# Head softmax: two blocks' denominators as one product, half of it behind the values; experts' sums in a shared bank, openings 16 units ahead

## The chip, the cores and the metric

The kernel runs on one core of a Trainium2 chip. The metric is the device time of one execution in microseconds (us), as the median of the runs shown. The core has five engines with queues of their own: PE (matrix products; PEld are its weight loads), DVE (vector), ACT (activations), POOL (elementwise work and some transfers) and SP (transfers).

## The reference

The program is a two-layer hybrid network on x of shape (2, 1024, 128) in float32. Only its last two steps matter here: an attention whose softmax runs over the heads, and a feed-forward layer of eight experts that is applied before it and again after it.

```python
# _L1_attn_b: 16 heads of 8
qkv = x @ w_qkv + b_qkv                    # -> q, k, v: (b, 16, n, 8)
dp = jnp.einsum('bhqd,bhkd->bhqk', q, k) * SCALE
attn = jax.nn.softmax(dp, axis=1)          # over the heads
w_avg = jnp.einsum('bhqk,bhkd->bhqd', attn, v)
out = w_avg.reshape(b, n, 128) @ w_proj + b_proj

# _L1_ffn: for each of 8 experts, FFN = 512
h = jax.nn.silu(x @ wg) * (x @ wu)
acc = acc + h @ wd
```

x takes the result of each step as an addition: x = x + ffn(x), x = x + attn_b(x), x = x + ffn(x).

## The kernel before

x lies in the on-chip memory as 16 tiles of 128 tokens (`x_res`). Earlier stages (latent attention, state space, linear attention) fill the first half of the execution. Then come `experts_ffn(g, w, [2])` (the experts on four tiles at once), `heads_and_experts(g, w, [6, 7], [0, 1, 2, 3, 4, 5])`, which the change touches, and `experts_ffn(g, w, [3])`.

`heads_and_experts` weaves two streams. The first is the head softmax. A block is 128 queries by 128 keys of all 16 heads; there are 2 x 8 x 8 = 128 blocks. For each block PE forms the scores in four banks (`products`, L1148), DVE takes the maxima over the heads (L1159) and subtracts them (L1165), and ACT takes the exponentials (L1168). The sum over 16 heads is then made in two steps: a transfer from SP's queue copies the lower eight heads (L1174), a transfer from POOL's queue adds the upper eight onto them (L1178), and PE adds the eight remaining slices with eight products by the identity (L1183). DVE inverts (L1188), POOL multiplies all heads by the inverse (L1193), and PE weighs the values (L1199). Eight blocks give one tile of 128 queries: ACT copies the result out (L1294), PE projects it (L1263) and DVE adds it to x (L1272). `finished` counts these tiles.

The second stream, `ExpertStream`, works on chunks of two tiles. A chunk is opened by five steps (norm statistics on DVE, root on ACT, inverse on DVE, norm on POOL, transposes on PE), and then gives 32 units (8 experts x 4 slices of FFN). A unit is two gate products on PE (L997), a SiLU on ACT (L1004), a product on DVE (L1012) and the output product (L1023). The outputs of two units at a time are added up in a bank, which DVE adds to x (L1032).

The order is written out by hand (`manual_schedule`): each engine executes the loop's instructions in the order of the code. Chunk 6 is worked off beside `preparation(0)`, the projections q, k, v of the first batch; chunk 7 and then 0 to 5 go through the block loop, two units an iteration. `aside(place)` slips in one step of an opening, or of `preparation(1)`, at its place. An opening begins when few enough units are left (the second number in `side`) and enough tiles are finished (the first). In iteration i the loop treats scores of block i+1, exponentials of i+1, the upper transfer of i, the denominators of i-1, the inverse and the multiplication of i-2 and the values of i-3.

Buffers: scores four banks once (`h_ps_s`), one bank `h_ps_d` for denominators, outputs and projection alike, one for the weighed values (`h_po`), two for gates (`e_pgu`); `h_e` has four buffers of 8 KB a partition, `h_a` two, `h_e2` three.

Of the kernel before, what the change touches and what calls it, by code (L numbers as in the profile page):

```python
# [19 lines left out]
P = 128  # L20
B = 2
L = 1024
# [932 lines left out]
class ExpertStream:  # L955

    NE, FC = 8, 4

    def __init__(self, g, w, work, ps):
        self.g, self.w, self.work, self.ps = g, w, work, ps
        self.units, self.fresh, self.gated, self.ready, self.sums = [], [], [], [], []

    def tokens(self, chunk):
        return self.g.x[:, 2 * chunk : 2 * chunk + 2, :]

# [20 lines left out]
    def products(self):  # L988

        nc, w = self.g.nc, self.w  # L990
        for _ in range(2):
# [16 lines left out]
    def multiply(self):  # L1008
        nc = self.g.nc
        for chunk, e, fc, pgu, sg in self.gated:  # L1010
            h = self.work.tile([P, 2 * P], F32, name="e_h", bufs=6)
            nc.vector.tensor_mul(h, sg, pgu[:, 1, :])  # L1012
            self.ready.append((chunk, e, fc, h))
        self.gated = []

    def outputs(self, po):

        nc = self.g.nc
        if self.ready:
            two, self.ready = self.ready[:2], self.ready[2:]  # L1020
            for t in range(2):
                for k, (_, e, fc, h) in enumerate(two):
                    nc.tensor.matmul(  # L1023
                        po[:, t, :], h[:, bass.ts(t, P)], self.w["Wd"][:, e, fc, :], start=(k == 0), stop=(k == 1)
                    )
            self.sums.append((two[0][0], po))

    def add(self):

        for chunk, po in self.sums:  # L1030
            xt = self.tokens(chunk)
            self.g.nc.vector.tensor_add(xt, xt, po[:, 0:2, :])  # L1032
        self.sums = []
# [12 lines left out]
def heads_and_experts(g, w, first, second):  # L1046
# [4 lines left out]
    with ExitStack() as es:  # L1051
# [10 lines left out]

        keep = one.tile([P, K], F32, name="h_keep")
# [12 lines left out]
        ex = ExpertStream(g, w, ework, ps_e)  # L1076
        qzs, kTs, vs = {}, {}, {}

        def preparation(b):
# [3 lines left out]
            u = seq.tile([P, TPB, D], F32, name="h_u", bufs=1)  # L1083
            uT = seq.tile([P, L], F32, name="h_uT", bufs=1)
            qzs[b] = seq.tile([P, K, L], F32, name="h_qz")
# [6 lines left out]
            for t in range(0, TPB, 2):  # L1092
                yield "pool", lambda t=t: ln.apply(u, (t, t + 1))

# [5 lines left out]

            def transposes(n):
                pt = ps_e.tile([P, 4, P], F32, name="e_pgu")
                for t in range(4):
                    nc.tensor.transpose(pt[:, t, :], u[:, 4 * n + t, :], g.ident)
                nc.scalar.copy(uT[:, bass.ts(n, 512)], pt.rearrange("p a b -> p (a b)"))

            def query(n):
                cols = bass.ts(n, 512)
                pm = ps_e.tile([P, 4, P], F32, name="e_pgu").rearrange("p a b -> p (a b)")
                nc.tensor.matmul(pm, w["w_qkv2"][:, 0:P], uT[:, cols], start=True, stop=True)  # L1110
                for k in range(K):
                    nc.scalar.activation(  # L1112
                        qzs[b][:, k, cols], pm, AF.Identity, bias=keep_b[:, k : k + 1], scale=keep[:, k : k + 1]
                    )

# [16 lines left out]
            for step in (transposes, key, query, value):  # L1132
# [10 lines left out]
        def products(b, qb, kb):  # L1143

            s = ps_s.tile([P, J, 512], F32, name="h_s")
            for j in range(J):
# [4 lines left out]
                    qzs[b][quad, :, bass.ts(qb, P)],  # L1151
# [10 lines left out]
        def exponentials(heads, m):  # L1162

            e = work.tile([P, H, P], F32, name="h_e", bufs=4)
# [7 lines left out]
        def lower(e):  # L1172
            e2 = work.tile([P, 8, P], F32, name="h_e2", bufs=3)
            nc.sync.dma_start(out=e2, in_=e[:, 0:8, :])  # L1174
            return e2
# [4 lines left out]
        def denominators(e2):  # L1180
            pd = ps_d.tile([P, 4, D], F32, name="h_pd")[:, 0, :]
            for k in range(8):
                nc.tensor.matmul(pd, g.ident, e2[:, k, :], start=(k == 0), stop=(k == 7))  # L1183
            return pd

        def inverse(pd):
            r = work.tile([P, P], F32, name="h_r")
# [3 lines left out]
        def normalize(e, r):  # L1191
            a = work.tile([P, H, P], F32, name="h_a")
            nc.gpsimd.tensor_mul(a, e, r.unsqueeze(1).to_broadcast([P, H, P]))  # L1193
            return a

        def weigh(kb, a, po):
            for k in range(K):
                for j in range(J):
# [4 lines left out]
                        start=(kb == 0 and k == 0),  # L1203
                        stop=(kb == TPB - 1 and k == K - 1),
                    )
# [3 lines left out]
        side = [(2 * c + 2, 8, ex.opening(c)) for c in second]  # L1209
        side.insert(1, (0, 24, preparation(1)))  # L1210
        side = [(0, 8, ex.opening(c)) for c in first[1:]] + side
# [28 lines left out]
        with tc.manual_schedule(engines=ALL):  # L1240
            for _, step in ex.opening(first[0]):
                step()
            for place, step in preparation(0):
                step()
                if place != "act":
                    po = ps_d.tile([P, 4, D], F32, name="h_pd")
                    ex.outputs(po)
                    ex.add()
# [4 lines left out]
            e_, e2_, d_, a_ = {}, {}, {}, {}  # L1253
            oT = po = None
            for i in range(-1, n + 4):
                if i + 1 < n:
                    heads = products(*blocks[i + 1])
                r = inverse(d_.pop(i - 2)) if 0 <= i - 2 < n else None
                if ex.ready or oT is not None:
                    pd = ps_d.tile([P, 4, D], F32, name="h_pd")  # L1260
                    ex.outputs(pd)
                    if oT is not None:
                        nc.tensor.matmul(pd[:, 2, :], oT, w["w_proj2"], start=True, stop=True)  # L1263
                ex.multiply()
                if not aside("pe"):
                    ex.products()
                if i + 1 < n:
                    m = maxima(heads)
                ex.add()
                if oT is not None:  # L1270
                    xt = g.x[:, finished, :]
                    nc.vector.tensor_add(xt, xt, pd[:, 2, :])  # L1272
# [3 lines left out]
                if i + 1 < n:  # L1276
                    e_[i + 1] = exponentials(heads, m)
                    e2_[i + 1] = lower(e_[i + 1])
                aside("dve")
                if 0 <= i - 1 < n:  # L1280
# [238 lines left out]
```

## Time and profile before

| what | us |
|---|---|
| median of 3 runs (lowest to highest) | 2267.17 (2259.31 to 2271.51) |
| the profiled execution | 2268.1 |
| its span in the profile | 2266.4 |
| first gate product of `heads_and_experts` (PE L997) | 1188.66 |
| first and last maxima of the block loop (DVE L1159) | 1252.30 and 2139.74 |
| PE busy over the span | 1974.6 |
| DVE busy over the span | 1694.8 |
| POOL busy over the span | 908.5 |
| POOL's multiplication by the inverse (L1193), 128 times | 583.0, mean 4.555 |

Times in the profile are counted from the start of the span. A row of the timeline or of a chain gives start, length, engine, line, and how many instruction records it holds; in brackets stands how long the engine was idle before it and what ended that. A group's row gives the count, busy time, the mean in ns, and the idle time before its instructions.

### The profile page before, as it was taken

To read this page: it belongs to the slowest core of one execution; us is meant where nothing else is said; L and a number is where in the kernel's file an instruction comes from. 1 tells how busy PE (TensorE), PEld (TensorE's weight loads), DVE (VectorE), ACT (ScalarE), POOL (GpSimd) and SP (SyncE) were. 2 spreads that over 40 slices of the span, in tenths; PEclk is the share of its full clock that TensorE was granted. 3 is DMA by queue.
4 is the path that set the end of the run, shared out by engine and by line. 5 is a ranking of instruction groups with operands and counts; after the bars stand their busy time and mean duration, and the time that the engine had idled before them with its cause. 6 is when DMAs were issued, how large, how long until landed. Compare 5 with 4: busy or idle time off the path is not lost. (4 is left out here: it accounts for less than half of the span.)

```text
span 2266.4 us, 36372 instructions
## 1 busy us (share of the span) xinstructions
PE 1974.6 (87%) x14832; PEld 1157.8 (51%) x14832; DVE 1694.8 (75%) x2054; ACT 1188.3 (52%) x1497; POOL 908.5 (40%) x480
## 2 busy tenths in 40 slices
PE   7679888779967558899898798988999999999999
PEld 4223343223334123344446576766777777777753
DVE  5966767897856789945323898988898899998822
ACT  1026512366624637734223675756777777777722
POOL 0013300063401020100101578887787777787720
PEclk9889988889988769999999899999999999999999
DMA  3000000395730577500000455565555555555500
GB/s 88 1 1 1 1 1 6 88 224 142 174 112 10 138 186 167 131 0 0 1 0 1 121 150 154 151 162 139 160 150 154 149 150 152 156 153 143 153 11 5
DMA packets 73798, 220.15 MB, mean 97 GB/s; under 512 B 9184, under 2 KB 19872, under 8 KB 73504
## 3 DMA queue, kind: packets, MB, share of 16 engines
q1 hardware_dynamic: 54736, 149.40, 22.0%
q0 software_dynamic: 18432, 67.12, 15.1%
q8 instruction: 116, 1.90, 0.4%
q10 hardware_dynamic: 464, 1.33, 0.3%
q14 instruction: 50, 0.41, 0.1%
HBM read 78.35 MB, written 5.24 MB: 37 GB/s over the span
## 5 line engine op out<-in xcount | busy, mean ns | idle before, releaser
L1193 POOL TENSOR_TENSOR h_a<-h_e,h_r 128x2048 f32<-128x2048 f32 x128 | 583.0, 4555 | 140.6 <-PE h_po L1199 100.2
L1159 DVE TENSOR_REDUCE h_m<-h_s 128x128 f32<-128x2048 f32 x128 | 293.2, 2291 | 70.9 <-PE h_s L1148 70.9
L1183 PE MATMUL h_pd<-h_e,ident 128*128 128x128 f32 x2048 | 264.7, 283 | 37.9 <-DMA h_e<-h_e 24.6
L1165 DVE TENSOR_TENSOR h_e<-h_s,h_m 128x2048 f32<-128x2048 f32 x128 | 292.4, 2284 | 2.3 <-DVE h_m L1159 0.6
L1168 ACT ACTIVATE h_e<-h_e 128x1024 f32<-128x1024 f32 x256 | 256.6, 1049 | 66.8 <-DVE h_e L1165 60.7
L1183 PEld LDWEIGHTS h_pd<-h_e,ident 128*128 128x128 f32 x2048 | 242.4, 194 | 80.6 <-DVE x_res L1032 47.6
L1004 ACT ACT_TABLE_LOAD x110 | 141.1, 1283 | 162.2 <-PE e_pgu L997 162.0
L356 POOL TENSOR_SCALAR_AFFINE_SELECT a_pT<-a_pT 128x256 f32<-128x256 f32 x120 | 125.9, 1072 | 223.3 <-ACT a_pT L353 137.5
L917 DVE TENSOR_TENSOR e_h<-e_sg,e_pu 128x512 f32<-128x512 f32 x128 | 87.0, 684 | 162.1 <-PE e_pu L910 136.4
L261 DVE TENSOR_REDUCE a_nm<-a_s 128x2 f32<-128x1024 f32 (+7 forms) x144 | 168.1, 1217 | 39.1 <-PE a_s L252 24.2
L912 ACT ACTIVATE e_sg<-e_pg 128x512 f32<-128x512 f32 x128 | 76.1, 596 | 191.1 <-PE e_pg L909 172.6
L1023 PEld LDWEIGHTS h_pd<-Wd,e_h 128*128 128x128 f32 x1024 | 125.1, 191 | 95.1 <-DVE e_h L1012 78.1
L353 ACT ACTIVATE a_pT<-a_st 128x1024 f32<-128x1024 f32 (+3 forms) x176 | 129.9, 792 | 72.8 <-PE a_st L339 72.0
L746 DVE TENSOR_TENSOR_SCAN s_h<-s_a,s_h 128x1024 f32<-128x1024 f32 x64 | 149.0, 2328 | 20.1 <-ACT s_a L714 15.4
L1148 PE MATMUL h_s<-h_qz,h_kT 32*128 32x512 f32 x1024 | 148.9, 651 | 17.1 <-DVE h_e L1165 12.1
L997 PE MATMUL e_pgu<-e_uT,Wg 128*128 128x256 f32 x512 | 155.0, 385 | 2.6 <-ACT h_qz L1112 2.1
L910 PE MATMUL e_pu<-e_uT,Wu 128*128 128x512 f32 x256 | 139.1, 626 | 19.5 <-DVE e_h L917 19.5
L1023 PE MATMUL h_pd<-Wd,e_h 128*128 128x128 f32 x1024 | 149.7, 288 | 6.6 <-DVE e_h L1012 3.6
L1178 POOL DMA_DIRECT2D h_e<-h_e x128 | 114.9, 898 | 100.8 <-DVE h_m L1159 48.7
L243 PE MATMUL a_s<-a_latT,a_qT 32*128 32x512 f32 (+3 forms) x768 | 117.7, 590 | 41.3 <-DVE a_nm L261 39.2
L997 PE MATMUL e_pgu<-e_uT,Wu 128*128 128x256 f32 x512 | 153.2, 381 | 0.0
L1168 ACT ACT_TABLE_LOAD x111 | 142.4, 1283 | 12.0 <-issue 7.7
(268 smaller groups left out, 3235.8 us busy)
## 6 DMA issues: line engine op xcount, KB each, us to landing
h_e<-h_e SPq DMA_DIRECT2D x128, 512.0 KB, 3.8
h_e<-h_e POOLq DMA_DIRECT2D x128, 512.0 KB, 4.5
s_a<-s_steps SPq DMA_DIRECT2D x64, 512.0 KB, 4.9
s_h<-s_steps SPq DMA_DIRECT2D x64, 512.0 KB, 6.4
s_steps<-s_gate SPq DMA_DIRECT2D x8, 256.0 KB, 3.6
Wg<-in_Wg_dram SPq DMA_DIRECT2D x8, 256.0 KB, 6.0
Wu<-in_Wu_dram SPq DMA_DIRECT2D x8, 256.0 KB, 5.9
Wd<-in_Wd_dram SPq DMA_DIRECT2D x8, 256.0 KB, 6.1
```

The lines of the kernel that those rows point to most:

```text
L261: nc.vector.tensor_reduce(nm[:, half, i, h : h + together], s[:, :, :n], AX.X, ALU.max, negate=True)
L746: nc.vector.tensor_tensor_scan(h, a, h, 0.0, ALU.mult, ALU.add)
L910: nc.tensor.matmul(pu, w["Wu"][:, e, f], opened[n], start=True, stop=True)
L997: nc.tensor.matmul(pgu[:, k, :], w[name][:, e, f], uT, start=True, stop=True)
L1004: nc.scalar.activation(sg, pgu[:, 0, :], AF.Silu)
L1023: nc.tensor.matmul(po[:, t, :], h[:, bass.ts(t, P)], self.w["Wd"][:, e, fc, :], start=(k == 0), stop=(k == 1))
L1148: nc.tensor.matmul(s[:, j, :].rearrange("p (k q) -> p k q", k=K), kTs[b][quad, bass.ts(kb, P)], qzs[b][quad, :, bass.ts(qb, P)], start=Tru ...
L1159: nc.vector.tensor_reduce(m, heads.rearrange("p h q -> p q h"), AX.X, ALU.max)
L1165: nc.vector.tensor_sub(e, heads, m.unsqueeze(1).to_broadcast([P, H, P]))
L1168: nc.scalar.activation(eh, eh, AF.Exp, scale=scale)
L1183: nc.tensor.matmul(pd, g.ident, e2[:, k, :], start=(k == 0), stop=(k == 7))
L1193: nc.gpsimd.tensor_mul(a, e, r.unsqueeze(1).to_broadcast([P, H, P]))
```

## The change

Denominators are now formed for two blocks, an even one and the next, in one product of 256 columns; `h_e2` becomes a pair of two. The eight products by the identity are issued in two halves, the first at the end of an even iteration behind the values, the second in the following odd iteration ahead of the values. The inverse is taken for both blocks at the start of the next even iteration. The multiplication by the inverse now writes in place, and comes two iterations later than before, as do the values. `h_e` has seven buffers.

The experts' outputs of a chunk are summed over all 32 units in one half of a bank, with the expert weights as the stationary operand, so that the sum is transposed; at its end ACT copies it out and zeroes it, PE transposes it back (`turn`) and DVE adds it to x once. The same bank (`held`) holds the weighed values and the projection; it is zeroed by ACT before the loops and after each tile, and the products in it accumulate. Where a tile is projected, the outputs come behind the gates. Where an opening's or preparation's PE step or a turn takes place, one unit is still given.

Openings may begin with 16 units left instead of 8. Preparation keeps four norm tiles at a time instead of eight and queries in pieces of 512 columns, and some weights of earlier stages move to a pool that is closed by then.

```diff
@@ class ExpertStream
-    def products(self):
+    def products(self, count=2):
...
-        for _ in range(2):
+        for _ in range(count):
...
-            h = self.work.tile([P, 2 * P], F32, name="e_h", bufs=6)
+            h = self.work.tile([P, 2 * P], F32, name="e_h", bufs=4)
...
-    def outputs(self, po):
+    def outputs(self):
         nc = self.g.nc
-        if self.ready:
-            two, self.ready = self.ready[:2], self.ready[2:]
+        two, self.ready = self.ready[:2], self.ready[2:]
+        for chunk, e, fc, h in two:
+            last = e == self.NE - 1 and fc == self.FC - 1
+            nc.tensor.matmul(
+                self.sums, self.w["Wd"][:, e, fc, :], h, start=False, stop=last, skip_group_check=True
+            )
+            if last:
+                oT = self.work.tile([P, 2 * P], F32, name="e_oT", bufs=1)
+                nc.scalar.copy(oT, self.sums)
+                nc.scalar.copy(self.sums, self.zero.to_broadcast([P, 2 * P]))
+                self.summed.append((chunk, oT))
+    def turn(self):
+        nc = self.g.nc
+        if self.done:
+            chunk, oT = self.done.pop(0)
+            pt = self.ps.tile([P, 4, P], F32, name="e_pgu")
             for t in range(2):
-                for k, (_, e, fc, h) in enumerate(two):
-                    nc.tensor.matmul(
-                        po[:, t, :], h[:, bass.ts(t, P)], self.w["Wd"][:, e, fc, :], start=(k == 0), stop=(k == 1)
-                    )
-            self.sums.append((two[0][0], po))
-    def add(self):
-        for chunk, po in self.sums:
+                nc.tensor.transpose(pt[:, t, :], oT[:, bass.ts(t, P)], self.g.ident)
             xt = self.tokens(chunk)
-            self.g.nc.vector.tensor_add(xt, xt, po[:, 0:2, :])
-        self.sums = []
+            nc.vector.tensor_add(xt, xt, pt[:, 0:2, :])
+            return True
+        self.done, self.summed = self.summed, []
+        return False
@@ heads_and_experts
+        zero = one.tile([P, 1], F32, name="h_zero")
+        nc.vector.memset(zero, 0.0)
+        held = ps_o.tile([P, 4 * P], F32, name="h_po")
+        sums, po, proj = held[:, 0 : 2 * P], held[:, 2 * P : 3 * P], held[:, 3 * P :]
...
-            u = seq.tile([P, TPB, D], F32, name="h_u", bufs=1)
             uT = seq.tile([P, L], F32, name="h_uT", bufs=1)
-            qzs[b] = seq.tile([P, K, L], F32, name="h_qz")
+            qzs[b] = []
...
-            for t in range(0, TPB, 2):
-                yield "pool", lambda t=t: ln.apply(u, (t, t + 1))
...
+            us = {}
+            def normalized(t):
+                if t % 4 == 0:
+                    us[t // 4] = seq.tile([P, 4, D], F32, name="h_u", bufs=1)
+                for k in (t, t + 1):
+                    nc.gpsimd.tensor_scalar(
+                        us[t // 4][:, k % 4, :], xb[:, k, :], ln.mv[:, k, 0:1], ln.rs[:, k : k + 1], ALU.subtract, ALU.mult
+                    )
...
-                    nc.tensor.transpose(pt[:, t, :], u[:, 4 * n + t, :], g.ident)
+                    nc.tensor.transpose(pt[:, t, :], us[n][:, t, :], g.ident)
...
+                qz = seq.tile([P, K, 512], F32, name="h_qz", bufs=3)
...
-            for step in (transposes, key, query, value):
+            for n in range(2):
+                for t in (4 * n, 4 * n + 2):
+                    yield "pool", lambda t=t: normalized(t)
+                yield "pe", lambda n=n: transposes(n)
+            for step in (key, query, value):
                 for n in range(2):
                     yield "pe", lambda step=step, n=n: step(n)
...
-            e = work.tile([P, H, P], F32, name="h_e", bufs=4)
+            e = work.tile([P, H, P], F32, name="h_e", bufs=7)
...
-            e2 = work.tile([P, 8, P], F32, name="h_e2", bufs=3)
+        def lower(e2, e):
             nc.sync.dma_start(out=e2, in_=e[:, 0:8, :])
-            return e2
         def upper(e2, e):
             nc.gpsimd.dma_start(out=e2, in_=e[:, 8:16, :], accum_op=ALU.add)
-        def denominators(e2):
-            pd = ps_d.tile([P, 4, D], F32, name="h_pd")[:, 0, :]
-            for k in range(8):
-                nc.tensor.matmul(pd, g.ident, e2[:, k, :], start=(k == 0), stop=(k == 7))
-            return pd
+        def denominators(pd, pair, half):
+            for k in range(4 * half, 4 * half + 4):
+                nc.tensor.matmul(pd, g.ident, pair[:, :, k, :], start=(k == 0), stop=(k == 7))
         def inverse(pd):
-            r = work.tile([P, P], F32, name="h_r")
+            r = work.tile([P, 2, P], F32, name="h_r")
             nc.vector.reciprocal(r, pd)
             return r
         def normalize(e, r):
-            a = work.tile([P, H, P], F32, name="h_a")
-            nc.gpsimd.tensor_mul(a, e, r.unsqueeze(1).to_broadcast([P, H, P]))
-            return a
-        def weigh(kb, a, po):
+            nc.gpsimd.tensor_mul(e, e, r.unsqueeze(1).to_broadcast([P, H, P]))
+        def weigh(kb, a):
             for k in range(K):
                 for j in range(J):
                     nc.tensor.matmul(
                         po[32 * j : 32 * j + 32, :],
                         vz[:, kb * J + j, k].rearrange("p a d -> p (a d)"),
                         a[:, 4 * j + k, :],
-                        start=(kb == 0 and k == 0),
+                        start=False,
                         stop=(kb == TPB - 1 and k == K - 1),
+                        skip_group_check=True,
                     )
-        side = [(2 * c + 2, 8, ex.opening(c)) for c in second]
+        side = [(2 * c + 2, 16, ex.opening(c)) for c in second]
         side.insert(1, (0, 24, preparation(1)))
-        side = [(0, 8, ex.opening(c)) for c in first[1:]] + side
+        side = [(0, 16, ex.opening(c)) for c in first[1:]] + side
...
         with tc.manual_schedule(engines=ALL):
+            nc.scalar.copy(held, zero.to_broadcast([P, 4 * P]))
             for _, step in ex.opening(first[0]):
                 step()
             for place, step in preparation(0):
                 step()
                 if place != "act":
-                    po = ps_d.tile([P, 4, D], F32, name="h_pd")
-                    ex.outputs(po)
-                    ex.add()
+                    ex.outputs()
+                    ex.turn()
                     ex.products()
                     ex.gates()
                     ex.multiply()
             spread(0)
-            e_, e2_, d_, a_ = {}, {}, {}, {}
-            oT = po = None
-            for i in range(-1, n + 4):
+            e_, pairs, d_, r_ = {}, {}, {}, {}
+            oT = None
+            for i in range(-1, n + 6):
                 if i + 1 < n:
                     heads = products(*blocks[i + 1])
-                r = inverse(d_.pop(i - 2)) if 0 <= i - 2 < n else None
-                if ex.ready or oT is not None:
-                    pd = ps_d.tile([P, 4, D], F32, name="h_pd")
-                    ex.outputs(pd)
-                    if oT is not None:
-                        nc.tensor.matmul(pd[:, 2, :], oT, w["w_proj2"], start=True, stop=True)
+                even = i % 2 == 0
+                if even and 0 <= i - 4 < n:
+                    r_[i - 4] = inverse(d_.pop(i - 4))
+                if oT is None:
+                    ex.outputs()
                 ex.multiply()
-                if not aside("pe"):
-                    ex.products()
+                ex.products(1 if ex.turn() or aside("pe") else 2)
+                if oT is not None:
+                    ex.outputs()
+                    nc.tensor.matmul(proj, oT, w["w_proj2"], start=False, stop=True, skip_group_check=True)
                 if i + 1 < n:
                     m = maxima(heads)
-                ex.add()
                 if oT is not None:
                     xt = g.x[:, finished, :]
-                    nc.vector.tensor_add(xt, xt, pd[:, 2, :])
+                    nc.vector.tensor_add(xt, xt, proj)
                     finished, oT = finished + 1, None
                 aside("act")
                 ex.gates()
                 if i + 1 < n:
                     e_[i + 1] = exponentials(heads, m)
-                    e2_[i + 1] = lower(e_[i + 1])
+                    if not even:
+                        pairs[i + 1] = work.tile([P, 2, 8, P], F32, name="h_e2")
+                    lower(pairs[i + 1 - even][:, int(even)], e_[i + 1])
                 aside("dve")
-                if 0 <= i - 1 < n:
-                    d_[i - 1] = denominators(e2_.pop(i - 1))
-                if r is not None:
-                    a_[i - 2] = normalize(e_.pop(i - 2), r)
+                pair = i - 2 if even else i - 3
+                if not even and 0 <= pair < n:
+                    denominators(d_[pair], pairs.pop(pair), 1)
+                if 0 <= i - 4 < n:
+                    normalize(e_[i - 4], r_[i - 4 - i % 2][:, i % 2, :])
                 if 0 <= i < n:
-                    upper(e2_[i], e_[i])
+                    upper(pairs[i - i % 2][:, i % 2], e_[i])
                 aside("pool")
-                if 0 <= i - 3 < n:
-                    b, qb, kb = blocks[i - 3]
-                    if kb == 0:
-                        po = ps_o.tile([P, P], F32, name="h_po")
-                    weigh(kb, a_.pop(i - 3), po)
+                if 0 <= i - 5 < n:
+                    b, qb, kb = blocks[i - 5]
+                    weigh(kb, e_.pop(i - 5))
                     if kb == TPB - 1:
                         oT = work.tile([P, P], F32, name="h_oT")
                         nc.scalar.copy(oT, po)
+                        nc.scalar.copy(held[:, 2 * P :], zero.to_broadcast([P, 2 * P]))
                         if qb == TPB - 1 and b + 1 < B:
                             spread(b + 1)
-            while ex.units or ex.fresh or ex.gated or ex.ready or side or current:
+                if even and 0 <= pair < n:
+                    d_[pair] = ps_d.tile([P, 2, P], F32, name="h_pd")
+                    denominators(d_[pair], pairs[pair], 0)
+            while ex.busy() or side or current:
                 while any([aside(place) for place in ("dve", "act", "pool", "pe")]):
                     pass
-                po = ps_d.tile([P, 4, D], F32, name="h_pd")
-                ex.outputs(po)
-                ex.add()
+                ex.outputs()
+                ex.turn()
                 ex.products()
                 ex.gates()
                 ex.multiply()
@@ tile_hybrid_kernel
-    for name in ("gamma", "beta", "w_qkv1", "w_out1", "w_qkv2", "w_proj2"):
+    for name in ("gamma", "beta", "w_qkv1", "w_out1"):
+        w[name] = g.load(name, d[name], list(d[name].shape), pool=early)
+    for name in ("w_qkv2", "w_proj2"):
         w[name] = g.load(name, d[name], list(d[name].shape))
...
-    for name in ("b_out1", "b_v2", "b_proj2"):
+    w["b_out1"] = g.load("b_out1", d["b_out1"].partition_broadcast(P), [P, D], pool=early)
+    for name in ("b_v2", "b_proj2"):
         w[name] = g.load(name, d[name].partition_broadcast(P), [P, D])
```

More of the change, by code (lines that the diff above doesn't have):

```diff
@@ L959, with __init__, busy @@
     NE, FC = 8, 4
-    def __init__(self, g, w, work, ps):
-        self.g, self.w, self.work, self.ps = g, w, work, ps
-        self.units, self.fresh, self.gated, self.ready, self.sums = [], [], [], [], []
+    def __init__(self, g, w, work, ps, sums, zero):
+        self.g, self.w, self.work, self.ps, self.sums, self.zero = g, w, work, ps, sums, zero
+        self.units, self.fresh, self.gated, self.ready, self.summed, self.done = [], [], [], [], [], []
     def tokens(self, chunk):
         return self.g.x[:, 2 * chunk : 2 * chunk + 2, :]
+    def busy(self):
+        return self.units or self.fresh or self.gated or self.ready or self.summed or self.done
     def opening(self, chunk):
@@ L1075, in heads_and_experts @@
         nc.gpsimd.memset(vz, 0.0)
-        ex = ExpertStream(g, w, ework, ps_e)
+        ex = ExpertStream(g, w, ework, ps_e, sums, zero)
         qzs, kTs, vs = {}, {}, {}
@@ L1110, in query @@
                 nc.tensor.matmul(pm, w["w_qkv2"][:, 0:P], uT[:, cols], start=True, stop=True)
+                qz = seq.tile([P, K, 512], F32, name="h_qz", bufs=3)
                 for k in range(K):
                     nc.scalar.activation(
-                        qzs[b][:, k, cols], pm, AF.Identity, bias=keep_b[:, k : k + 1], scale=keep[:, k : k + 1]
+                        qz[:, k, :], pm, AF.Identity, bias=keep_b[:, k : k + 1], scale=keep[:, k : k + 1]
                     )
+                qzs[b].append(qz)
             def key(n):
@@ L1150, in products @@
                     kTs[b][quad, bass.ts(kb, P)],
-                    qzs[b][quad, :, bass.ts(qb, P)],
+                    qzs[b][qb // 4][quad, :, bass.ts(qb % 4, P)],
                     start=True,
@@ L1169, in exponentials @@
             return e
-        def lower(e):
-            e2 = work.tile([P, 8, P], F32, name="h_e2", bufs=3)
+        def lower(e2, e):
             nc.sync.dma_start(out=e2, in_=e[:, 0:8, :])
-            return e2
         def upper(e2, e):
             nc.gpsimd.dma_start(out=e2, in_=e[:, 8:16, :], accum_op=ALU.add)
-        def denominators(e2):
-            pd = ps_d.tile([P, 4, D], F32, name="h_pd")[:, 0, :]
-            for k in range(8):
-                nc.tensor.matmul(pd, g.ident, e2[:, k, :], start=(k == 0), stop=(k == 7))
-            return pd
+        def denominators(pd, pair, half):
+            for k in range(4 * half, 4 * half + 4):
+                nc.tensor.matmul(pd, g.ident, pair[:, :, k, :], start=(k == 0), stop=(k == 7))
         def inverse(pd):
-            r = work.tile([P, P], F32, name="h_r")
+            r = work.tile([P, 2, P], F32, name="h_r")
             nc.vector.reciprocal(r, pd)
```

## The prediction

> **What bounds the kernel now.** I read the page's busy shares first, then busy time by stretch, then the chain of work that ended last, then the timeline of one light iteration, PE's list of waits, and two groups. The change touches only the head softmax stage with the experts woven into it, from about 1187 to 2170 us.
>
> ```profile
> 1600.00:1800.00 200.00, 195.49 (x2070) 151.25 (x2072) 183.57 (x183) 150.11 (x180) 157.83 (x63) 1.00 0.58 154
> 1800.00:2000.00 200.00, 194.17 (x2026) 149.22 (x2019) 180.47 (x175) 147.43 (x172) 156.18 (x59) 1.00 0.58 154
> ```
>
> The columns are length, busy PE, PEld, DVE, ACT, POOL, granted clock, DMA share. PE is busy 97% and DVE 92%: two engines lie near the limit, and a gain on PE can be worth only what DVE leaves. One iteration in the chain:
>
> ```profile
> 1709.82 1.07 PE h_s L1148 x8
> 1710.89 1.09 PE h_pd L1023 x8
> 1711.98 1.73 PE e_pgu L997 x8
> 1713.70 1.98 PE h_pd L1183 x16
> 1715.68 1.01 PE h_po L1199 x32
> ```
>
> Nothing but PE: 1.07 + 1.09 + 1.73 + 1.98 + 1.01 = 6.88 us, and successive maxima (L1159) are indeed 6.87 apart. A float32 matmul leaves two records, so 16 records are 8 products. A 128-wide product costs 1.98 / 8 = 0.247, or 0.272 in the experts' outputs; a 256-wide one 1.73 / 4 = 0.433. Where PE has less to do, the timeline shows the next limit:
>
> ```profile
> 1403.82 2.29 DVE L1159 TENSOR_REDUCE h_m<-h_s 128x128 f32<-128x2048 f32 x1 [2.15 <-PE h_s L1148]
> ...
> 1406.20 2.29 DVE L1165 TENSOR_TENSOR h_e<-h_s,h_m 128x2048 f32<-128x2048 f32 x1
> ...
> 1408.64 1.14 PE L1148 MATMUL h_s<-h_qz,h_kT 32*128 32x512 f32 x8 [0.79 <-DVE h_e L1165]
> ...
> 1409.84 2.29 DVE L1159 TENSOR_REDUCE h_m<-h_s 128x128 f32<-128x2048 f32 x1 [0.48 <-PE h_s L1148]
> ```
>
> Scores have one buffer, so this loop is closed: 2.38 to the subtraction, 2.44 to the next scores, 1.20 to the next maxima, together 6.02. Only 2.44 - 2.21 + 1.20 = 1.43 of it is free for DVE's other work.
>
> ```profile
> PE h_pd L1183 <- DMA h_e<-h_e: 22.4, 23, 2.8
> PE h_s L1148 <- DVE h_e L1165: 12.1, 7, 4.8
> PE h_pd L1183 <- DVE x_res L1032: 10.0, 8, 1.7
> ...
> PE h_pd L1183 <- DVE x_res L1272: 2.6, 2, 1.7
> ```
>
> These are PE's waits between 1252 and 2140 (total, times, longest).
>
> **The change part by part.** *Denominators.* Per two blocks, 16 products of 0.247 become 8 of 0.433: 1.98 falls to 1.73 a block. *Experts' outputs.* Four of 0.272 become two of 0.433: 1.09 falls to 0.87. PE's iteration is then 1.07 + 0.87 + 1.73 + 1.73 + 1.01 = 6.41. A rule speaks against this gain: the Trainium skill, "TensorE: Matmul & The Clock Gate", section "Back-to-back issue gap", gives isolated matmuls their streaming time plus 2.5 ns. Merging two would save 2 x 2.5 = 5 ns a pair, 0.02 + 0.01 us an iteration, some 4 us over 128. The rows give 2 x 0.247 - 0.433 = 61 ns a pair and 0.47 an iteration, 60 in all. I take the rows, which are this stage's own.
>
> *DVE.* The 128 additions into x (L1032, 0.41 each) become 8. Reciprocals are done for two blocks at once:
>
> ```profile
> L1188 DVE RECIPROCAL h_r<-h_pd 128x128 f32<-128x128 f32 x128 | 122.0, 953 | 23.4 <-PE h_pd L1183 23.3
> ...
> L69 DVE RECIPROCAL h_rs<-h_rs 128x8 f32<-128x8 f32 x2 | 0.4, 198 | 1.2 <-ACT h_rs L66 1.2
> ```
>
> The slope is (953 - 198) / 120 = 6.3 ns an element, so 256 take 1.76, of which 0.07 overlaps its neighbour: 1.69. Twice the row would be 1.91. All of it stands in even iterations, ahead of the maxima: there DVE needs 2.21 subtraction + 1.69 + 0.62 for two gates' products + 2.38 maxima = 6.90, over PE's 6.41. Odd iterations are the closed loop, 6.02. The pair is 12.92, or 6.46 a block; PE's pair of 12.82 just fits. So DVE becomes the bound, and about 105 full iterations gain 6.88 - 6.46 = 0.42: **-44**.
>
> *Waits removed.* Products no longer share a bank with the additions: the 10.0 + 2.6 us of waits on x go: **-13**. But DVE's norm statistics, hidden now, lie on the bound: seven openings of 4 x 0.23 + 0.15 and a preparation of 3.8: **+11**.
>
> *Turn.* Six times inside the loop, two transposes (2 x 0.25) and one addition come before the maxima: those start at 1.07 + 0.87 + 0.50 + 0.20 + 0.33 = 2.97 after the scores' start instead of 1.7. Behind them are subtraction, exponentials and the next scores: about 1.2 each, **+7**. *Projection,* 15 times. It moves behind gates and outputs, 1.07 + 1.73 + 0.87 + 0.25 + 0.20 = 4.12, and its addition (0.28) holds the subtraction, otherwise due at 3.58: +0.82 where it costs 0.25 now: **+9**. *Light and filling iterations:* some twenty pay half of a 1.69 reciprocal on a 6.02 loop, and the values of preparation stand behind an output: **+7**.
>
> *Shared bank.* The skill's "PSUM — Partial Sum Buffer", section "PSUM bank collisions raise a hardware error", asks that a bank be guarded whole. The changed program does: after a weighed sum, PE's outputs wait for ACT's copy and zeroing, two instructions queued after the exponentials. By the rule alone 24 such events would each stop PE for 0.27 + 0.37 + 0.2: 20 us. By the rows exponentials end 2.0 after the scores' start, the bank is free at 2.8 to 2.9, and PE, given the gates first, arrives at 2.80: 2 us or less. I take 1 and keep both ends.
>
> *DMA waits.* The second block's upper half is issued 7.5 us after its pair's even subtraction and lands 4.6 later (medians 3.9 and 4.5 for the two transfers): 12.1. The first half of the product, now behind the values, comes at 13.5: slack 1.4, as now, but 64 appointments replace 128. Of 22.4 us I take away 8 (between 0 and 22). The three-deep-to-seven-deep score buffers remove no wait that shows. POOL has 4.53 + 0.88 + 0.13 = 5.54 of 6.46, so the multiplication in place stays covered; if that cover went, 0.1 a block would cost 13. An opening 16 units ahead asks for the same steps; I give it nothing (0 to -5).
>
> *Start.* The order of the changed program puts ACT's zeroing of the shared bank ahead of the first opening's root (L66). That zeroing waits for the bank, and so for the end of the previous experts stage; now root, inverse and POOL's norm run hidden behind that stage. New chain: x's last addition ends 1188.7, the zero 1188.9, DVE's masks 0.46 + 2.54 to 1191.9, inverse 0.16, two POOL norms of 0.88 to 1193.8, transposes and copy 0.9: first gate at 1194.8 instead of 1188.66, **+6**. PE is then idle for six microseconds. After such a gap of 3 to 4 us the trace shows half rate for some 6 us (L909's 0.85 instead of 0.43 from 2174.98): **+2**. Sixteen turns of the run-in save 0.23 each, and its closing turn costs 1.2: **-3**.
>
> *End.* Values come two blocks later. From the last maxima R (2139.74): the last upper lands at R + 15, the first half of the pair's product ends at R + 16.8, output, gates and second half at R + 21.1, reciprocal at R + 23, two multiplications of 4.53 at R + 32.1. Now the last ends at R + 24.7 and values start at R + 26.7: **+5** (to +8).
>
> Sum: -44 - 13 + 11 + 7 + 9 + 7 + 1 - 8 + 6 + 2 - 3 + 5 = -20. The profiled execution took 2268.1 (span 2266.4), so 2248; the median of the runs lies 0.9 below it: **2247**.
>
> **The rivals.** *A, more gain, 2222:* DMA waits (14 more of the 22) and half-clock stretches vanish, and start and end cost half. For: PE's waits and slow clock before are some 60 us. Against: PE's and DVE's pairs differ by 0.1 only, so any disturbance still shows. *B, eaten up, 2264:* the reciprocal takes 1.91 (0.11 a block, 12), DMA waits stay (8), turn and projection cost a little more; the 0.42 is spent. For: these are many small terms of one sign. Against: each was read from a row. *C, slower, 2286:* one mechanism, the pair's product waiting for the accumulating transfer at the end of even iterations. It decides once lower plus upper take over 1.4 us more than 3.9 + 4.6; at 2.0 more, 0.6 for each of 64 pairs is +38 to 2285. For: the trace's longest landings are 6.1 and 6.6, and the pace is quicker. Against: the medians.
>
> **How the numbers follow.** Likeliest (2236 to 2256): 0.48. A: 0.14. B: 0.25. C: 0.13. The range reaches into A and B to leave out two in ten: 2228 to 2271. A measurement of this kernel tells 0.5% (11 us) from no change: below 2256 faster, 0.62; to 2278 same, 0.25; above slower, 0.13.
>
> **What would show it.** Maxima alternately 6.9 and 6.0 apart; denominators and outputs at 0.43 a product; the reciprocal at 1.76; DVE nearer 95% than PE in the middle; the first gate some 6 us later against the stage before; the last values about 32 us after the last maxima. It is wrong if maxima are 6.4 apart throughout (DVE hides the reciprocal), or if PE's wait on the transfers exceeds 22 us.

## The result, and the profile after

The changed kernel takes 2285.01 us (median of 5 runs, 2282.30 to 2288.66) against 2267.17: a ratio of 1.0068, with a 95% interval of 1.0049 to 1.0086. It is 18 us slower; the forecast was 20 us faster. Its profiled execution spans 2284.9 us.

First the place. The maxima stand at the head of every block, so I cut the stage at them. From the first to the last maxima lay 887.4 us before (1252.30 to 2139.74) and lie 892.4 after (1259.16 to 2151.57): +5.0, where the forecast's loop terms make -30. The first maxima come 6.9 later (forecast +5). Of these 6.9, 1.3 lie ahead of the change: the last addition into x of the stage before starts at 1189.32 instead of 1188.03. Measured from there the first gate comes 5.7 later (6.33 instead of 0.63) and the first maxima 5.6 later. From the last maxima to the end of the span it is 133.3 instead of 126.7, +6.7 (forecast +5). So start and end were right, and some 35 us are missing in the loop.

```profile
1189.32 0.69 DVE L932 TENSOR_TENSOR x_res<-x_res,e_pu 128x512 f32<-128x512 f32 x1 [3.22 <-PE e_pu L114]
1195.65 1.22 PE L1002 MATMUL e_pgu<-e_uT,Wg 128*128 128x256 f32 x2 [0.46 <-ACT e_uT L988]
```

Busy time by stretch in the changed kernel, for the same two stretches that the prediction shows of the kernel before. The columns are length, busy PE, PEld, DVE, ACT and POOL (with instruction counts), granted clock, DMA share, GB/s:

```profile
1600.00:1800.00 200.00, 191.35 (x1729) 135.79 (x1728) 175.87 (x142) 158.41 (x189) 158.58 (x63) 1.00 0.61 155
1800.00:2000.00 200.00, 191.44 (x1726) 136.04 (x1725) 174.24 (x139) 155.15 (x185) 157.31 (x59) 1.00 0.60 153
```

PE is still busy 96%, with some 15% fewer instructions; DVE, which was forecast to become the bound, fell from 92% and 90% to 88% and 87%. So PE has fewer products and hardly less to do. PE's timeline of a full pair of iterations shows it (start, length, line, operation; what counts is the distance from one start to the next):

```profile
1332.21 1.13 PE L1027 MATMUL h_po<-e_h,Wd 128*128 128x256 f32 x4
1333.18 0.59 PE L1002 MATMUL e_pgu<-e_uT,Wg 128*128 128x256 f32 x2
...
1335.00 1.08 PE L1228 MATMUL h_po<-h_e,h_vz 128*32 128x128 f32 x32
1336.01 1.99 PE L1215 MATMUL h_pd<-h_e,ident 128*128 128x256 f32 x8
1337.94 1.14 PE L1183 MATMUL h_s<-h_qz,h_kT 32*128 32x512 f32 x8
1339.01 1.13 PE L1027 MATMUL h_po<-e_h,Wd 128*128 128x256 f32 x4
1339.97 0.59 PE L1002 MATMUL e_pgu<-e_uT,Wg 128*128 128x256 f32 x2
...
1341.70 1.89 PE L1215 MATMUL h_pd<-h_e,ident 128*128 128x256 f32 x8
1343.52 1.08 PE L1228 MATMUL h_po<-h_e,h_vz 128*32 128x128 f32 x32
1344.53 1.14 PE L1183 MATMUL h_s<-h_qz,h_kT 32*128 32x512 f32 x8
```

Even iteration: outputs 0.97, gates 1.82, values 1.01, half product 1.93, scores 1.07: 6.80. Odd: outputs 0.96, gates 1.73, half product 1.82, values 1.01, scores 1.07: 6.59. A pair takes 13.39, so the mean is 6.70, not 6.41, and PE never stops in it. The same distances in the kernel before:

```profile
1849.66 1.14 PE L1148 MATMUL h_s<-h_qz,h_kT 32*128 32x512 f32 x8
1850.73 1.16 PE L1023 MATMUL h_pd<-Wd,e_h 128*128 128x128 f32 x8
1851.72 0.60 PE L997 MATMUL e_pgu<-e_uT,Wg 128*128 128x256 f32 x2
...
1853.54 2.05 PE L1183 MATMUL h_pd<-h_e,ident 128*128 128x128 f32 x16
1855.52 1.08 PE L1199 MATMUL h_po<-h_a,h_vz 128*32 128x128 f32 x32
1856.53 1.14 PE L1148 MATMUL h_s<-h_qz,h_kT 32*128 32x512 f32 x8
```

Here outputs take 0.99, gates 1.82, denominators 1.98. The outputs fell by 0.02 a block and not by 0.22; the denominators, two blocks together, from 3.96 to 3.75, of which an even iteration gives 0.1 back in its gates.

PE's two longest waits between the first and the last maxima of the changed kernel (total, times, longest):

```profile
PE h_pd L1215 <- DMA h_e<-h_e: 26.3, 20, 4.4
PE h_s L1183 <- DVE h_e L1200: 23.9, 16, 4.8
```

The waits on x (10.0 and 2.6 before) are gone, as forecast. Those on transfers rose from 22.4 to 26.3, though half as many products ask for one, and those for the subtraction from 12.1 to 23.9. The longest comes where PE has no expert units:

```profile
1387.28 1.08 PE L1228 MATMUL h_po<-h_e,h_vz 128*32 128x128 f32 x32
1392.79 3.75 PE L1215 MATMUL h_pd<-h_e,ident 128*128 128x256 f32 x8 [4.43 <-DMA h_e<-h_e]
```

The upper half that it waits for was issued at 1385.37 and landed 7.3 us later. After the 4.43 of waiting the half product takes 3.68 instead of 1.93, at a granted clock of 0.50 (1392.70 to 1396.50). So one late transfer cost this iteration over 5 us (11.26 between its maxima). In all 20 waits it is the upper half of the pair's odd block that lands last, 0.14 us before PE starts.

What DVE was to do came out as forecast:

```profile
L1219 DVE RECIPROCAL h_r<-h_pd 128x256 f32<-128x256 f32 x64 | 111.7, 1745 | 16.8 <-PE h_pd L1215 16.7
```

It takes 1.745 (forecast 1.76), and where nothing disturbs, even maxima are 6.86 apart (forecast 6.90). Odd ones are 6.53 in full iterations, not 6.02: there DVE waits for PE's scores.

### The profile page after: what moved, and what is told of

Its sections match the earlier page's. It is cut to its first block, busy times and chain, and to the rows that moved or that the text cites. A ratio compares the mean times of both kernels' runs of the same rounds, so it can differ in the third digit from the quotient of the medians.

```text
span 2284.9 us, 33040 instructions
## 1 busy us (share of the span) xinstructions
PE 1969.9 (86%) x13312; PEld 1094.9 (48%) x13312; DVE 1654.0 (72%) x1871; ACT 1238.6 (54%) x1557; POOL 913.0 (40%) x480
## 5 line engine op out<-in xcount | busy, mean ns | idle before, releaser
L1223 POOL TENSOR_TENSOR h_e<-h_e,h_r 128x2048 f32<-128x2048 f32 x128 | 602.2, 4707 | 79.3 <-issue 70.9
L1194 DVE TENSOR_REDUCE h_m<-h_s 128x128 f32<-128x2048 f32 x128 | 292.6, 2286 | 83.2 <-PE h_s L1183 83.2
L1215 PE MATMUL h_pd<-h_e,ident 128*128 128x256 f32 x1024 | 254.2, 392 | 28.1 <-DMA h_e<-h_e 27.8
L1215 PEld LDWEIGHTS h_pd<-h_e,ident 128*128 128x128 f32 x1024 | 192.6, 194 | 65.7 <-issue 37.3
L1183 PE MATMUL h_s<-h_qz,h_kT 32*128 32x512 f32 x1024 | 149.3, 651 | 30.0 <-DVE h_e L1200 23.9
L1027 PE MATMUL h_po<-e_h,Wd 128*128 128x256 f32 x512 | 148.3, 405 | 6.7 <-ACT h_po L1033 3.5
L1228 PE MATMUL h_po<-h_e,h_vz 128*32 128x128 f32 x4096 | 140.5, 279 | 5.4 <-POOL h_e L1223 5.4
```

Of the source, the lines that this page charges most:

```text
L1027: nc.tensor.matmul(self.sums, self.w["Wd"][:, e, fc, :], h, start=False, stop=last, skip_group_check=True)
L1183: nc.tensor.matmul(s[:, j, :].rearrange("p (k q) -> p k q", k=K), kTs[b][quad, bass.ts(kb, P)], qzs[b][qb // 4][quad, :, bass.ts(qb % 4, P ...
L1194: nc.vector.tensor_reduce(m, heads.rearrange("p h q -> p q h"), AX.X, ALU.max)
L1215: nc.tensor.matmul(pd, g.ident, pair[:, :, k, :], start=(k == 0), stop=(k == 7))
L1223: nc.gpsimd.tensor_mul(e, e, r.unsqueeze(1).to_broadcast([P, H, P]))
```

## The experiments

Two causes stand beside each other: T, the transfers' appointments are missed; R, turn, projection and other work ahead of the maxima cost more than the forecast gave them. A third, on the size of PE's products, came up after the first four kernels. Ratios are to the kernel before on the same chip, with 95% intervals; "loop" is from the first to the last maxima of the profiled execution, to be set against 887.4 before and 892.4 after. A profiled execution is one run of several and can lie up to 9 us from the median: that of the experts' part alone took 2271.55, the shortest of its eight.

**The accumulating transfers left out.**

```
                 if 0 <= i < n:
-                    upper(pairs[i - i % 2][:, i % 2], e_[i])
```

> The changed kernel without the accumulating transfers: the denominators then add up only the lower eight heads of each block, and the upper eight are left out. Nothing else differs; PE's pair of products waits for the plain copy alone. Theory T (the some 30 us that the forecast missed are PE's waits for the accumulating transfer of the odd block, with the half clock and the late scores that follow them): the 28 us of waits go and the half clock after them, 2285 falls to 2240 to 2255. Rival R (the loss is in what stands before the maxima and the subtraction: turn, projection, the longer reciprocal; the transfers cost no more than before): at least 2272.

Measured: 2263.47, ratio 0.9970 (0.9960 to 0.9981); loop 869.8. Against the changed kernel's 1.0068 it is 0.0098 less, 22 us. (POOL's issue and the traffic go too, so this is the price of the whole chain.) The forecast had kept 14 us of the transfers' waits, so this is 8 of the 35 that were missed. R's 2272 is ruled out, but T's 2255 isn't reached either. With no transfer to wait for, full iterations still alternate 6.86 and 6.53. So the clean pace itself had been put too fast.

**The experts' part alone.** Denominators per block, four score buffers, reciprocal and multiplication as in the kernel before; outputs, turn and shared bank as changed.

```
-                    denominators(d_[pair], pairs[pair], 0)
+                    d_[i - 1] = denominators(e2_.pop(i - 1))
...
-            e = work.tile([P, H, P], F32, name="h_e", bufs=7)
+            e = work.tile([P, H, P], F32, name="h_e", bufs=4)
```

> The changed kernel with the denominators, the score buffers and the multiplication put back as they were, so that only the experts' sums in the shared bank, the openings at 16 and the split preparation are left. Outputs 0.87, denominators 1.98: PE's iteration 6.66. T: the loss belongs to the pairs, so by the forecast's terms -23 -13 +11 +7 +9 +1 +6 -3 = -5, 2262 (2255 to 2270). R: turn, projection and start are all here, so it loses as the changed kernel does, 2275 to 2290.

Measured: 2280.24, ratio 1.0050 (1.0033 to 1.0068); loop 891.8. T as I had put it there, that the loss belongs to the pairs, falls: the pairs add 0.0018, less than the intervals tell. R's 2275 to 2290 holds the result, but the rows show another cause than R's. PE's timeline of this kernel:

```profile
1837.00 0.59 PE L1002 MATMUL e_pgu<-e_uT,Wg 128*128 128x256 f32 x2
...
1838.73 1.95 PE L1218 MATMUL h_pd<-h_e,ident 128*128 128x128 f32 x16
1840.60 1.08 PE L1234 MATMUL h_po<-h_a,h_vz 128*32 128x128 f32 x32
```

Gates 1.73 and denominators 1.87 instead of 1.82 and 1.98, and its undisturbed maxima are 6.65 apart. That this meets the expected 6.66 is luck: outputs take 0.97 and not 0.87, denominators 1.87 and not 1.98. With products 128 wide it is as quick as the pairs are. And its waits:

```profile
PE h_pd L1218 <- DMA h_e<-h_e: 36.1, 40, 2.7
```

40 waits where the kernel before had 23. PE, quicker here too, waits more often for the transfers, pairs or not.

**The turn's addition behind the subtraction**, in the changed kernel. `turn` keeps its result, and `land`, called behind the exponentials, adds it to x.

```
-            nc.vector.tensor_add(xt, xt, pt[:, 0:2, :])
+            self.turned = (chunk, pt)
...
+                ex.land()
```

> The changed kernel with the turn's addition into x issued behind the subtraction on DVE instead of before the maxima. Six to eight turn iterations of 9.3 us should fall to 7.5. T: 5 to 9 us of the whole, 2276 to 2280. R: the late maxima are what makes the transfers late, so 12 to 20 us, 2265 to 2273.

Measured: 2280.62, ratio 1.0064 (1.0040 to 1.0089); loop 887.7. Set against 1.0068 nothing is to be seen, and T's 2280 is missed by little. The turn's own iterations fell from 9.3 to 7.7 or 7.9, but one three to six later rose (7.84 for 6.12, 7.31 for 6.10, 7.76 for 6.54), and the waits on transfers from 26.3 to 32.1. R's 12 to 20 are ruled out, and what was freed was lost again in later iterations, with longer waits on transfers.

**Openings at 8 units instead of 16.**

> The changed kernel with openings and preparation asked for as in the kernel before, at 8 units left instead of 16. T: PE's empty iterations, in which it reaches the pair's product before the transfer, get no fewer: 2283 to 2292. R: no effect beyond 3 us, 2282 to 2288.

Measured: 2289.89, ratio 1.0090 (1.0071 to 1.0109); loop 895.6. Opening earlier gives some 5 us by the ratios, the far end of the forecast's "0 to -5", but the two intervals overlap, and T and R can't be told apart by it.

**Every product of the pair in two.**

```
-                nc.tensor.matmul(pd, g.ident, pair[:, :, k, :], start=(k == 0), stop=(k == 7))
+                for t in range(2):
+                    nc.tensor.matmul(pd[:, t, :], g.ident, pair[:, t, k, :], start=(k + t == 0), stop=(k == 7), skip_group_check=True)
```

> The changed kernel with every 256-wide denominator product written as two 128-wide ones, at the same two places. Account W (the forecast's: a pair of 128-wide products costs 61 ns more than one of 256): 8 x 0.061 = 0.49 a pair of blocks, over some 52 full pairs +25, about 2310. Account G (a 128-wide product is 0.222 and a 256-wide 0.433, so the width is worth 11 ns, and what costs is a change between groups of products): 0.09 a pair, +5, 2286 to 2293.

Measured: 2289.33, ratio 1.0095 (1.0069 to 1.0121): 6 us above the changed kernel by the ratios, which is within the intervals. W's 2310 is ruled out. Its timeline:

```profile
1859.32 1.95 PE L1216 MATMUL h_pd<-h_e,ident 128*128 128x128 f32 x16
1861.20 1.08 PE L1229 MATMUL h_po<-h_e,h_vz 128*32 128x128 f32 x32
```

Eight 128-wide products take 1.88, four 256-wide ones at the same place 1.82: 0.06 a half, 15 ns a merged pair, and not 61.

**The first half ahead of the values**, without accumulating transfers. The lines come from behind the values.

```
+                if even and 0 <= pair < n:
+                    d_[pair] = ps_d.tile([P, 2, P], F32, name="h_pd")
+                    denominators(d_[pair], pairs[pair], 0)
                 if 0 <= i - 5 < n:
                     b, qb, kb = blocks[i - 5]
                     weigh(kb, e_.pop(i - 5))
```

> The kernel without the accumulating transfers (the upper eight heads are left out of the denominators), with the first half of the pair's product ahead of the values in even iterations instead of behind them. G: two changes between full products and the 32-wide ones of values and scores fewer, about 0.2 a pair, so even PE iterations of 6.6 instead of 6.8 and 8 to 12 us less than the 2263 of the kernel it is compared with: 2250 to 2256. W: a place has no price on PE, 2261 to 2266.

Measured: 2254.61, ratio 0.9940 (0.9921 to 0.9959), 7 to 9 us below the 2263 (ratio 0.9970). Its timeline, two half products in a row:

```profile
1840.84 1.89 PE L1215 MATMUL h_pd<-h_e,ident 128*128 128x256 f32 x8
1842.66 1.08 PE L1228 MATMUL h_po<-h_e,h_vz 128*32 128x128 f32 x32
1843.67 1.14 PE L1183 MATMUL h_s<-h_qz,h_kT 32*128 32x512 f32 x8
...
1847.00 1.89 PE L1215 MATMUL h_pd<-h_e,ident 128*128 128x256 f32 x8
1848.82 1.08 PE L1228 MATMUL h_po<-h_e,h_vz 128*32 128x128 f32 x32
```

Both halves now take 1.82, and full maxima alternate 6.86 and 6.34 instead of 6.86 and 6.53. The place behind the values cost 0.2 a pair.

**The first zeroing behind the first opening**, in the changed kernel.

```
-            nc.scalar.copy(held, zero.to_broadcast([P, 4 * P]))
             for _, step in ex.opening(first[0]):
                 step()
+            nc.scalar.copy(held, zero.to_broadcast([P, 4 * P]))
```

> The changed kernel with the first zeroing of the shared bank issued behind the first opening instead of before it, so that the opening's root, inverse and norm can run while the stage before ends. By the forecast's account of the start: 4 to 6 us less, 2279 to 2281, and the first maxima as early as before. If ACT's zeroing is not what holds the opening: no difference, 2283 to 2287.

Measured: 2279.46, ratio 1.0048 (1.0032 to 1.0065). The interval overlaps the changed kernel's, so the rows decide:

```profile
1189.21 0.69 DVE L932 TENSOR_TENSOR x_res<-x_res,e_pu 128x512 f32<-128x512 f32 x1 [3.22 <-PE e_pgu L986]
1189.84 0.70 PE L1002 MATMUL e_pgu<-e_uT,Wg 128*128 128x256 f32 x2 [0.52 <-ACT e_uT L988]
```

The stage before ends as in the changed kernel, and the first gate comes 0.63 behind that addition, as before, instead of 6.33. The first maxima start at 1252.16 instead of 1259.16. The forecast's account of the start holds.

**One iteration more for the transfers**, with the experts' part alone.

```
-                if 0 <= i - 1 < n:
-                    d_[i - 1] = denominators(e2_.pop(i - 1))
+                if 0 <= i - 2 < n:
+                    d_[i - 2] = denominators(e2_.pop(i - 2))
```

Reciprocal, multiplication and values move one block with it; scores get five buffers and the half sums four.

> The kernel with the experts' part alone (denominators per block), with denominators, reciprocal, multiplication and values one iteration later each, so that every accumulating transfer has one iteration more. If the missed transfers are what eats the gain of the experts' part (34 us of waits on transfers there, and the half clock behind them): 2280 falls to 2246 to 2258. If turn, projection and empty iterations eat it: 2272 or more, with waits on the transfers gone all the same.

Measured: 2245.68, ratio 0.9894 (0.9866 to 0.9923); loop 858.3, against 891.8 without the extra iteration. PE's two longest waits:

```profile
PE h_s L1183 <- DVE h_e L1200: 21.5, 14, 4.8
PE h_s L1183 <- DVE ex_rs L69: 8.2, 3, 4.8
```

Its whole list of waits holds none on a transfer, although transfers got no shorter (medians 4.6 and 5.1). This is the plainest proof that late transfers ate the gain: 35 us come from moving an appointment. The same edit was not run on the pairs, where it needs an eighth score buffer of 8 KB a partition, nor on the kernel before.

**The first half ahead of the values with all transfers.** The edit is that of the kernel without accumulating transfers, made in the changed one.

> The changed kernel, all transfers in it, with the first half of the pair's product ahead of the values. PE saves the 0.2 a pair that it saved without the accumulating transfers (9 us there), but it asks for the odd block's transfer 1.0 us earlier. Theory T (the transfer's slack is used up): waits on transfers rise from 28 to over 50 us and the time is 2285 to 2310. If the transfers cost only in disturbed iterations, PE's saving stays: 2274 to 2278.

Measured: 2302.26, ratio 1.0139 (1.0113 to 1.0164); loop 905.4.

```profile
PE h_pd L1215 <- DMA h_e<-h_e: 43.3, 33, 5.5
```

The waits stay below the "over 50" that T expected; the time is as expected. An edit that saves PE 7 to 9 us where no transfer is late costs 16 where one is.

**Both repairs on the best kernel.** First the zeroing behind the opening, then the turn's addition behind the subtraction as well.

> The experts' part with denominators one iteration later, and with the first zeroing behind the first opening. The start's 5 to 6 us are independent of the loop: 2245.7 falls to 2240 (2238 to 2242).

> The same, and the turn's addition into x behind the subtraction. In the changed kernel that move gave nothing, since the iterations that it freed ended at the next wait on a transfer. If that is so, it must give its 6 x 1.2 = 7 us (the 9.4 + 6.0 of a turn become 13.3 to 14.0) where no transfer is waited for: 2231 to 2236. If the turn is hidden anyway: 2238 to 2242.

Measured: 2238.61, ratio 0.9857 (0.9831 to 0.9883), and 2232.73, ratio 0.9831 (0.9805 to 0.9857). The turn's move, worth nothing in the changed kernel, is worth some 6 us here; the two intervals overlap, but the rows bear it out: in four turns 9.38 + 6.01 become 7.79 + 6.06, and the loop falls from 858.4 to 852.2. The last kernel is 1.7% faster than the kernel before, and it has no pairs.

## Why the prediction was wrong

**The failed step is the size of PE's gain:** "Per two blocks, 16 products of 0.247 become 8 of 0.433 ... Four of 0.272 become two of 0.433", and against the rule "I take the rows". 0.247 was 1.98 / 8, the time of a whole group over its products. Start by start inside a group, a 128-wide float32 product takes 0.222 and a 256-wide one 0.433. Merging two saves 11 ns (15 in the kernel with split products), much nearer to the rule's 5 than to my 61. What else a group holds belongs to its edges, and for these the forecast's new iteration had nothing. A full product is one of 128 rows and 128 columns; scores use 32 rows, values 32 columns. Where PE goes from full products to scores or values, or back, the full products' group takes about 0.1 longer: the half product is 1.93 between values and scores and 1.82 between gates and values; gates take 1.82 ahead of values and 1.73 ahead of a half product; outputs take 0.97 behind scores, and 0.86 between gates and a projection, as here:

```profile
1865.46 1.03 PE L1027 MATMUL h_po<-e_h,Wd 128*128 128x256 f32 x4
1866.32 0.38 PE L1298 MATMUL h_po<-w_proj,h_oT 128*128 128x128 f32 x2
```

The kernel before has two such edges an iteration. The changed one has two in odd iterations and four in even ones, where half a product stands between values and scores. Six edges a pair make 0.57, and that is all of the difference between the measured pair of 13.39 and the forecast's 12.82. I missed the rule that fits: the Trainium skill, "TensorEngine Tiling (Array Packing)", section "Key Properties", says that changing the tiling mode drains TensorE. It gives no figure; these traces show 0.1 on the full products' side of each change, and moving the half product away from between the two took 0.2 a pair off. That it is a drain no run here shows. At such an edge the trace has the weight load start together with its product (both at 1336.01 for the half product above), and inside a group it starts ahead; a load that isn't hidden would look the same.

The denominators' group of before also held a wait. What PE and its weight loads waited for ahead of L1183, from the first maxima to the last:

```profile
  DVE x_res L1032: 57.3, 96
```

PE's own list has 10.0 of it, 8 times; the rest is weight loads held by a wait of the product that they belong to. In the experts' part alone, where denominators no longer share a bank with those additions, this wait is gone, and gates and denominators are 0.09 and 0.11 shorter. So most of the 0.22 that I gave to wider outputs exists, but by these rows it comes from the parted banks; no run parts the banks alone.

Full iterations are thus 6.88 before and 6.70 after, a gain of 0.18 and not 0.42: with the forecast's 105 full iterations I estimate -19 instead of -44, 25 us of the 35 missed.

**DMA waits** are the second term: "Of 22.4 us I take away 8". Leaving the accumulating transfers out gives 22 us, where the forecast had kept 14: 8 more; with 26.3 us of waits, over the 22 that the forecast named as a sign of being wrong. Rival C named the mechanism and priced the sum at 2286, with 0.13; but its condition, transfers over 1.4 us longer, did not hold. That its 2286 lies next to the measured 2285 is luck. The medians went from 3.8 and 4.5 to 4.6 and 4.7, 1.0 together. It was enough to miss some appointments: of 64 pairs 20 waited. Here is the slack, on POOL's timeline:

```profile
1861.88 0.88 POOL L1211 DMA_DIRECT2D h_e<-h_e  x1
1862.48 4.84 POOL L1223 TENSOR_TENSOR h_e<-h_e,h_r 128x2048 f32<-128x2048 f32 x1
1868.25 0.88 POOL L1211 DMA_DIRECT2D h_e<-h_e  x1 [0.93 <-DMA h_e<-h_e]
```

The odd block's upper half waits for its lower half; issued at 1868.25, it lands 4.5 us later, at 1872.8. PE's even iteration begins at 1869.46, and with 1.07 + 0.97 + 1.82 + 1.01 it asks at 1874.3. These 1.5 us, close to the forecast's 1.4, are less than the spread of the landings: upper halves took 4.5 to 7.3. The forecast had compared the slack with medians.

**Right:** the reciprocal, the even iterations on DVE, the waits on x, the start (5.6 against 5, shown by the moved zeroing), the end (6.7 against 5), projections (7.72 between maxima, 0.82 over 6.90). **The turn** was priced too low: with no transfer waited for, its two iterations take 9.38 + 6.01 = 15.39 against 13.30 for two undisturbed ones, 2.1 where the forecast had 1.2. Moving the addition takes 1.5 of it back; in the changed kernel that gain is lost again. **Shared bank:** 3.5 us in four waits of outputs and 2.3 in two of projections, where 1 was taken and 20 was the far end.

These terms overlap, and their sum is no closed account of the 35. One more is not parted from them: over the loop the granted clock was 0.98 before and 0.97 after, and 0.97 too without the accumulating transfers. Two readings of the prediction slipped without weight: the score buffers were four deep before, not three, and the lower half's median was 3.8, not 3.9.

The pair's ring of two doesn't slow the lower half. SyncE's queue does wait at L1208 for the pair's product before it (281.9 us in 62 waits), but each lower half is issued within 0.2 us of the end of the exponentials that it copies, nearly all within 0.03, as in the kernel before. Why the transfers take longer in the changed kernel stays open.

## What to carry to other kernels

Price a product by the distance between two starts inside its group, and the group's edges apart: a mean over the group puts waits and changes of array shape into a width that doesn't cause them. Before making a bound engine faster, look at what it will then meet too early: here much of what PE saved was lost to an accumulating transfer with some 1.5 us of slack, and giving that transfer one iteration more was worth 35 us in the kernel without pairs. An edit that shows nothing may be hidden by the next wait; try it again when that wait is gone.

## What the runs showed of the hardware

- A float32 product leaves two records, 0.111 apart at 128 columns and 0.216 at 256; the width was worth 0.01 us a merged pair.
- Each change between full and 32-row or 32-column products cost the full products' group about 0.1 (half product 1.93 with two changes, 1.82 with one).
- After 4.4 us without work PE ran the next 8 records at about half pace (3.68 for 1.93), at a granted clock of 0.50.
- POOL's multiplication in place takes 4.53 in even iterations and some 4.83 in odd ones (mean 4.71); out of place it was 4.56. Why was not tried; POOL is not the bound.
- Transfers of 512 KB landed in 3.8 (plain) and 4.5 (accumulating) before, 4.6 and 4.7 in the changed kernel, 4.6 and 5.1 in the one with an iteration more (medians, us).
